# Nine gather slots with four routes in place of ten with three, and adjacency reloads in four parts, in a two-layer graph kernel

## The chip, the cores and the metric

The kernel runs on one core of a Trainium2 chip. The metric is the device time of one execution in microseconds (us).

## The reference

Two layers on N = 4096 nodes with D = 512 features. Cut to what matters:

```python
# layer 0: normalized adjacency, x: (4096, 512), adj: (4096, 4096)
a = adj + eye(N);  d = sum(a, axis=1) ** -0.5
h = relu((d[:, None] * a * d[None, :]) @ x @ W.T + b)
x = layernorm(x + h)
# layer 1: attention of 8 heads, masked by the adjacency
adj = maximum(adj, eye(N))
scores = q @ k.T * kd ** -0.5 + 0.01 * eye(N) - 1e16 * (1 - adj)
x = layernorm(x + sum_over_heads(softmax(scores) @ v @ Wo))
```

The adjacency matrix has a diagonal and some 0.2% of the other entries, all of them below 1. With a mask of 1e16 * (1 - adj), softmax then gives each row its own diagonal, and layer 1 becomes a matrix product with the sum over heads of Wv Wo. Layer 0 needs the few edges of each row only.

## The kernel before

`few_edges_below_one` computes this short form, and at its end a flag `bad` that says whether the inputs allow it (all values below 1, no row segment with too many edges, every edge found a slot). If not, a general kernel runs after it.

The rows are 32 tiles of 128. Five compute engines' queues (PE, DVE, ACT, POOL and SP, which here only issues DMAs) each run in their own order; a tile framework puts in the waits and may move instructions of a queue past each other, except where `keep_in_program_order` is used.

**First stage** (to about 220 us). It loads all adjacency tiles (2 MB each), sums their rows for the degrees, forms y = d * (x W.T) tile by tile and writes y to DRAM. DVE meanwhile begins to extract edges: `extraction` takes for each of eight column segments of a tile the eight largest values (L731) and their places (L732), packs them into keys, sorts out the 24 largest per row, and writes a record `rec` (column, weight, destination row and their remainders in low precision). It handles 7 of a tile's 16 steps per iteration here, and the rest in the second stage. Twelve tiles are extracted early from their first load, five stay resident in SBUF, and the other fifteen (`again`) are loaded a second time in the second stage by `reload` (L535), each into one of the five slots of the pool `big` once an older tile in it is extracted and its negative sum taken (`scan_half`, L687, two halves per tile on ACT).

**Matching.** A row may have more edges than KH = 10 slots. Rows of a tile are ranked by their number of edges (`match_key` L808, `match_across` L815, `match_ranks` L822), and a permutation matrix (`match_perm` L832) with products on PE (`match_move` L840 and L843) brings edges 10 to 23 of the fullest rows into free slots of emptier rows. The constant `sources` says which rank sends to which row; each of the three ROUTES moves a range of slots of the rows from one rank on. `match_end` (L851 to L858) writes the result to `wr_all` (column, weight, row distance, negated weight) and `cols_all`. The stages of this pipeline are issued at fixed steps k of an iteration.

**Second stage** (from about 220 us). Iteration i has KH steps k. In each, PE multiplies the gathered rows g of one slot by a 128x128 matrix s_t (L1265), POOL issues the indirect gather of a slot AHEAD = 18 slots later (L1057), and ACT builds one matrix of a later tile (`spread`, L955 to L968): for the first SAME = 5 slots a scaled identity, for the others a square and a relu that put each weight in its destination row. Around it stand, at steps given by `at`: `load_own` (L1067 and L540: own rows of y and x, two iterations ahead, three buffers), `own_part` (L1115, ACT), `own_bias` (L1119, DVE), `scaled` (L1126) and `residual` (L1137) on DVE at step 1 of the next iteration, four transposes and their copy hT (L663, L668) at step 0 two iterations behind, the product with wvo (`times`, L675) at step 6, the sum of squares (L1145), `variance` (L1156), `power` on POOL for two tiles at once (L1164), and `finish` (L1170 and L1171) for two tiles at once. The last two tiles (SUMMED) add up their first SAME slots on DVE and ACT before one product. The remaining extraction is shared out over 28 iterations (SPREAD). PSUM has eight banks: two for transposes, one (`bank`) for both `match_across` and `match_move`, five for products.

Of the kernel before, what the change touches and what calls it, by code (L numbers as in the profile page):

```python
# [9 lines left out]
FP = mybir.dt.float32  # L10
# [4 lines left out]
P = 128  # L15
# [404 lines left out]
def few_edges_below_one(  # L420
# [32 lines left out]
    KH = 10  # L453

    ROUTES = ((112, 10, 14), (120, 14, 19), (76, 19, 24))
    SAME = KH - max(hi - lo for _, lo, hi in ROUTES)

# [9 lines left out]
    ps_a = ctx.enter_context(tc.tile_pool(name="ps_a", bufs=5, space=bass.MemoryType.PSUM))  # L467
# [34 lines left out]
    for n, (c, _, _) in enumerate(ROUTES):  # L502
        ranks(sources[:, n + 1, : c + 1], -2, 2 * c + 1 - P)
        ranks(sources[:, n + 1, c + 1 :], -2, P - 1)
# [205 lines left out]
    def extraction(t, a_t, rec):  # L710
# [35 lines left out]
        def drop(f, r):  # L746
# [19 lines left out]
                lambda: nc.scalar.activation(  # L766
                    mask, keyf[:, 0], AF.Sign, accum_out=n_all[:, t : t + 1]
                ) if second else nc.vector.tensor_scalar(
                    mask, keyf[:, 0], 0.0, 0.0, op0=ALU.is_gt, op1=ALU.add,
                    accum_out=n_all[:, t : t + 1],  # L770
                ),
# [28 lines left out]
    bank = ps_t.tile([P, 512], FP, name="bank", bufs=1)  # L800
# [12 lines left out]
    def match_across(key):  # L813
        pk = bank[:, :P]
        tc.keep_in_program_order(nc.tensor.transpose(pk, key.to_broadcast([P, P]), ident))  # L815
        return pk
# [18 lines left out]
    def match_move(rec, perm):  # L835

        r = upper(rec)
        merged = bank[:, P : P + 7 * KH].rearrange("p (f k) -> p f k", f=7)
# [3 lines left out]
        for n, (_, lo, hi) in enumerate(ROUTES):  # L842
# [6 lines left out]
    def match_end(t, merged):  # L849
# [5 lines left out]
        if second:  # L855
            nc.scalar.activation(wr[:, 3], wr[:, 1], AF.Copy, scale=-1.0)
        else:
            nc.vector.tensor_scalar(wr[:, 3], wr[:, 1], -1.0, None, op0=ALU.mult)  # L858
# [42 lines left out]
    def steps():  # L901

        after = [[] for _ in range(STEPS)]
        for n, t in enumerate(order):
            if t not in a_tiles:
                reload()
            edges[t] = dict(rec=recs.tile([P, 7, K], FP, name="rec"))
# [32 lines left out]
    reloaded, scanned = [], []  # L940

    def reload():

        t = queue.pop(0)
        reloaded.append(t)
        a_tiles[t] = load_a(t)
# [100 lines left out]
    AHEAD = 18  # L1047
# [14 lines left out]
    def load_own(i):  # L1062
# [3 lines left out]
        yo[i] = p2.tile([P, D], FP, name="yo", bufs=3)  # L1066
        nc.sync.dma_start(yo[i], y[ts(t, P), :])  # L1067
        xs[i] = load_x(t, nc.sync, p2, 3)
# [42 lines left out]
    def own_part(i):  # L1111
        t = order[i]
        own = own_all[:, t : t + 1]
        d = d_all[:, t : t + 1]
        nc.scalar.activation(own, own, AF.Identity, scale=d, bias=d)  # L1115
# [15 lines left out]
    def residual(i, c=slice(0, D), part=0):  # L1131
        if i % 2 == 0 and i not in sts:
            sts[i] = small.tile([P, 2, 5], FP, name="sums")
            sts[i + 1] = sts[i][:, 1]
            pairs[i] = sts[i]
            sts[i] = sts[i][:, 0]
# [23 lines left out]
    def power(i, n):  # L1160

        j = i % 2
        st = pairs[i - j][:, j : j + n]
        nc.gpsimd.tensor_tensor(  # L1164
            st[:, :, 4], st[:, :, 3], mhalf.to_broadcast([P, n]) if n > 1 else mhalf, ALU.pow
        )
# [39 lines left out]
    yo, zs, hs, pts, hTs, ws, sts, pairs, mats, halves = ({} for _ in range(10))  # L1206
# [4 lines left out]
    load_own(1)  # L1211
    own_part(0)
# [8 lines left out]
    def at(step, i, k):  # L1221

        near = {"T": (1, 5), "M": (1, 8), "Q": (2, 2), "V": (2, 3), "F": (2, 7)}
        far = {"T": (2, 0), "M": (2, 6), "Q": (3, 1), "V": (3, 4), "F": (3, 8)}
        for table, tiles in ((near, range(NT - 2, NT)), (far, range(NT - 2))):
            behind, place = table[step]
            if k == place and i - behind in tiles:
                return i - behind
        return None

    for i in range(NT + 2):
# [5 lines left out]
        for k in range(KH):  # L1237
            ends = p == NT - 1
            t = at("T", i, k)
            if t not in (None, NT - 1):  # L1240
                hTs[t] = evacuate(p2, "hT", transpose_rows(hs[t]))
            t = at("M", i, k)
            if t not in (None, NT - 1):
                ws[t] = times(hTs.pop(t), wvo)
            if i == NT - 1:
# [3 lines left out]
                if k == 7:  # L1249
# [105 lines left out]
```

## Time and profile before

| | us |
|---|---|
| median of 3 runs | 749.92 |
| lowest, highest | 746.94, 760.13 |
| the profiled execution | 746.64 |
| its span, first to last instruction | 744.8 |

| engine | busy us | share of the span |
|---|---|---|
| PE | 591.2 | 79% |
| DVE | 545.4 | 73% |
| ACT | 525.2 | 71% |
| POOL | 393.2 | 53% |

The page has busy rows, the span in 40 slices (18.6 us each; a digit is the busy share in tenths), queues, and groups of instructions with their mean duration and what ended the idle time before them. PE is TensorE's matmul row and PEld its weight loads. An fp32 product of 128x512 has two records of each. In lists of waits, "A <- B: total, times, longest" says that the engine of A stood idle before A until B was done; "issue" and "remote" are idle times for which the profile shows no releaser. Shares are means over stages: the first stage and the second have different limits.

### The profile page before, as it was taken

To read this page: it belongs to the slowest core of one execution; us is meant where nothing else is said; L and a number is where in the kernel's file an instruction comes from. 1 tells how busy PE (TensorE), PEld (TensorE's weight loads), DVE (VectorE), ACT (ScalarE), POOL (GpSimd) and SP (SyncE) were. 2 spreads that over 40 slices of the span, in tenths; PEclk is the share of its full clock that TensorE was granted. 3 is DMA by queue.
4 is the path that set the end of the run, shared out by engine and by line. 5 is a ranking of instruction groups with operands and counts; after the bars stand their busy time and mean duration, and the time that the engine had idled before them with its cause. 6 is when DMAs were issued, how large, how long until landed. Compare 5 with 4: busy or idle time off the path is not lost. (4 is left out here: it accounts for less than half of the span.)

```text
span 744.8 us, 8023 instructions
## 1 busy us (share of the span) xinstructions
PE 591.2 (79%) x1638; PEld 273.9 (37%) x1638; DVE 545.4 (73%) x2109; ACT 525.2 (71%) x1152; POOL 393.2 (53%) x494
## 2 busy tenths in 40 slices
PE   1799959867815687989979699979996789898692
PEld 0444424433302233434434344434442334343350
DVE  6779899999997289889978799959994443322410
ACT  1787798958975287688958597867884887773432
POOL 3224233322337656766666666666665566667500
PEclk9999999999967778999999899999998899999896
DMA  8999999999947689999999988989996577777601
GB/s 341 403 422 426 425 423 406 421 430 413 423 187 262 198 294 366 343 371 373 380 305 343 325 300 313 337 297 333 351 333 209 171 221 239 224 240 248 199 24 62
DMA packets 54411, 230.54 MB, mean 310 GB/s; under 512 B 8592, under 2 KB 9616, under 8 KB 48080
## 3 DMA queue, kind: packets, MB, share of 16 engines
q0 software_dynamic: 30800, 100.95, 40.6%
q1 hardware_dynamic: 18416, 119.55, 40.5%
q10 hardware_dynamic: 5136, 9.44, 3.4%
q14 instruction: 44, 0.36, 0.1%
q8 instruction: 15, 0.25, 0.1%
HBM read 213.12 MB, written 16.78 MB: 309 GB/s over the span
## 5 line engine op out<-in xcount | busy, mean ns | idle before, releaser
L1057 POOL DMA_INDIRECT g<-y,cols_all x320 | 312.9, 978 | 151.0 <-issue 82.6
L1265 PE MATMUL acc<-g,s_t 128*128 128x512 f32 x600 | 283.6, 619 | 20.0 <-ACT s_t L959 20.0
L731 DVE MAX8 v_all<-a_t 128x8 f32<-128x512 f32 x256 | 168.8, 679 | 18.1 <-DMA a_t<-in_adj_dram 18.1
L732 DVE FIND_INDEX8 idx<-v_all,a_t 128x8 uint32<-128x512 f32 x256 | 174.0, 683 | 0.0
L1265 PEld LDWEIGHTS acc<-g,s_t 128*128 128x128 f32 x600 | 116.2, 200 | 151.9 <-issue 124.4
L675 PE MATMUL acc<-wvo,hT 128*128 128x512 f32 x256 | 125.4, 630 | 25.4 <-issue 14.8
L675 PE MATMUL acc<-wT,xT 128*128 128x512 f32 x256 | 121.7, 621 | 16.4 <-ACT xT L668 12.2
L687 ACT ACTIVATE dump<-a_t 128x2048 uint8<-128x2048 f32 (+1 forms) x52 | 119.5, 2297 | 0.0
L675 PEld LDWEIGHTS acc<-wvo,hT 128*128 128x128 f32 x256 | 49.1, 200 | 87.6 <-issue 71.9
L675 PEld LDWEIGHTS acc<-wT,xT 128*128 128x128 f32 x256 | 48.3, 198 | 72.3 <-issue 50.2
L955 ACT ACTIVATE sq<-cols,wr_all 128x128 f32<-128x128 f32 x192 | 66.9, 391 | 9.9 <-issue 7.3
L959 ACT ACTIVATE s_t<-sq,wr_all 128x128 f32<-128x128 f32 x160 | 72.0, 483 | 1.6 <-ACT sq L955 1.2
L968 ACT ACTIVATE s_t<-s_t,wr_all 128x128 f32<-128x128 f32 x150 | 52.4, 391 | 4.6 <-issue 3.8
L682 ACT ACTIVATE dump<-a_n 128x4096 uint8<-128x4096 f32 x15 | 54.5, 3632 | 0.3 <-DMA a_n<-in_adj_dram 0.3
L744 DVE MAX8 top<-key 128x8 f32<-128x64 f32 x192 | 39.0, 214 | 12.1 <-issue 7.3
L1119 DVE SCALAR_TENSOR_TENSOR yo<-yo,own_all,b_bc 128x512 f32<-128x512 f32 x32 | 23.8, 744 | 24.1 <-DMA yo<-y 10.4
L1126 DVE SCALAR_TENSOR_TENSOR h<-acc,d_all,yo 128x512 f32<-128x512 f32 (+1 forms) x33 | 23.9, 724 | 23.5 <-PE acc L1265 11.3
L540 POOL DMA_DIRECT2D x_t<-in_x_dram x32 | 17.9, 564 | 41.2 <-PE pt L663 41.0
L694 POOL TENSOR_SCALAR deg<-deg_all 128x1 f32<-128x1 f32 x32 | 6.7, 220 | 62.4 <-ACT dump L682 62.3
L704 POOL DMA_DIRECT2D y<-y_t x32 | 19.0, 593 | 38.6 <-ACT y_t L702 38.1
L702 ACT ACTIVATE y_t<-acc,d_all 128x512 f32<-128x512 f32 x32 | 21.6, 686 | 22.6 <-POOL d_all L697 16.7
L815 PE MATMUL bank<-ident,rank_key 128*128 128x128 f32 x32 | 10.2, 320 | 33.4 <-issue 11.5
(123 smaller groups left out, 651.5 us busy)
## 6 DMA issues: line engine op xcount, KB each, us to landing
a_t<-in_adj_dram SPq DMA_DIRECT2D x30, 2048.0 KB
a_n<-in_adj_dram SPq DMA_DIRECT2D x15, 2048.0 KB
x_t<-in_x_dram POOLq DMA_DIRECT2D x32, 256.0 KB
y<-y_t POOLq DMA_DIRECT2D x32, 256.0 KB
yo<-y SPq DMA_DIRECT2D x32, 256.0 KB
x_t<-in_x_dram SPq DMA_DIRECT2D x32, 256.0 KB
out_dram<-r_t ACTq DMA_DIRECT2D x32, 256.0 KB
g<-y,cols_all POOLq DMA_INDIRECT x320
```

Of the source, the lines that this page charges most:

```text
L675: nc.tensor.matmul(u, srcT[:, dc, :], w[:, dc, :], start=(dc == 0), stop=(dc == ND - 1))
L682: nc.scalar.activation(dump[:, : part.shape[1]], part, AF.Copy, accum_out=dst)
L687: nc.scalar.activation(dump[:, o], a_t[:, o], AF.Relu, scale=-1.0, accum_out=neg_all[:, t, halves[0] : halves[0] + 1],)
L731: long.append(lambda o=o, seg=seg: nc.vector.max(v[:, o], seg))
L732: long.append(lambda o=o, seg=seg: nc.vector.max_index(idx[:, o], v[:, o], seg))
L744: return lambda: nc.vector.max(top[:, f, r * 8 : r * 8 + 8], keyf[:, f])
L955: nc.scalar.activation(sq, cols1, AF.Square, bias=wr[:, 2, k : k + 1])
L959: nc.scalar.activation(s_t[:, k, :], away(), AF.Relu, scale=wr[:, 3, k : k + 1], bias=wr[:, 1, k : k + 1],)
L968: nc.scalar.activation(s_t[:, k, :], s_t[:, KH, :], AF.Copy, scale=wr[:, 1, k : k + 1])
L1057: nc.gpsimd.indirect_dma_start(out=slots[j], out_offset=None, in_=y[:, :], in_offset=bass.IndirectOffsetOnAxis(ap=cols_all[:, t, k : k + 1 ...
L1126: nc.vector.scalar_tensor_tensor(hs[i][:, c], zs[i][:, c], d_all[:, order[i] : order[i] + 1], yo[i][:, c], op0=ALU.mult, op1=ALU.add,)
L1265: nc.tensor.matmul(zs[i], mats[i][:, k, :], slots.pop(i * KH + k), start=(k == 0), stop=(k == KH - 1),)
```

## The change

- KH goes from 10 to 9, so each tile has nine gathers, nine products and nine steps per iteration. Four ROUTES replace three: edges 9 to 12, 13 to 15, 16 to 19 and 20 to 23. `sources` is filled with a value that matches no rank, and 22 runs of destination rows with their first source rank are written into it.
- `match_across` and `match_move` get PSUM tiles of their own, and the products have four banks.
- Some jobs of the second stage go from ACT to DVE: the count of edges (`mask`, L766), the negated weight (L856), and `own_part` (L1115).
- Transposes and their copy are three steps apart, `power` is taken per tile and at step 3, `finish` per tile at step 3 four iterations behind. `load_own` is three iterations ahead with four buffers. AHEAD is 16. The matching stages have other steps.
- A reload is booked at step 8 from iteration 2 on. Its four parts of 512 KB are issued at steps 0, 3, 5 and 7 from the next iteration on, or all at once before the extraction that needs the tile.

```diff
-    KH = 10
-    ROUTES = ((112, 10, 14), (120, 14, 19), (76, 19, 24))
-    SAME = KH - max(hi - lo for _, lo, hi in ROUTES)
+    KH = 9
+    ROUTES = (
+        (9, 13, ((62, 79, 54), (82, 89, 36), (91, 94, 28), (96, 96, 24), (99, 101, 23),
+                 (104, 107, 20), (110, 112, 16), (114, 127, 13))),
+        (13, 16, ((63, 65, 10), (66, 68, 13), (74, 75, 15), (80, 81, 7), (95, 95, 5), (97, 98, 4),
+                  (102, 103, 2), (108, 108, 0))),
+        (16, 20, ((61, 61, 4), (66, 66, 2), (90, 90, 1), (109, 109, 3), (113, 113, 0))),
+        (20, 24, ((109, 109, 0),)),
+    )
+    SAME = KH - max(hi - lo for lo, hi, _ in ROUTES)
...
-    ps_a = ctx.enter_context(tc.tile_pool(name="ps_a", bufs=5, space=bass.MemoryType.PSUM))
+    ps_a = ctx.enter_context(tc.tile_pool(name="ps_a", bufs=4, space=bass.MemoryType.PSUM))
...
-    for n, (c, _, _) in enumerate(ROUTES):
-        ranks(sources[:, n + 1, : c + 1], -2, 2 * c + 1 - P)
-        ranks(sources[:, n + 1, c + 1 :], -2, P - 1)
+    nc.gpsimd.memset(sources[:, 1:], float(P))
+    for n, (_, _, runs) in enumerate(ROUTES):
+        for a, b, r in runs:
+            ranks(sources[:, n + 1, a : b + 1], -2, 2 * r + 1 - P)
...
-                lambda: nc.scalar.activation(
-                    mask, keyf[:, 0], AF.Sign, accum_out=n_all[:, t : t + 1]
-                ) if second else nc.vector.tensor_scalar(
-                    mask, keyf[:, 0], 0.0, 0.0, op0=ALU.is_gt, op1=ALU.add,
-                    accum_out=n_all[:, t : t + 1],
-                ),
+                one(mask, keyf[:, 0], 0.0, 0.0, op0=ALU.is_gt, op1=ALU.add,
+                    accum_out=n_all[:, t : t + 1]),
...
-    bank = ps_t.tile([P, 512], FP, name="bank", bufs=1)
-        pk = bank[:, :P]
+        pk = ps_t.tile([P, 512], FP, name="pk", bufs=1)[:, :P]
-        merged = bank[:, P : P + 7 * KH].rearrange("p (f k) -> p f k", f=7)
+        pm = ps_t.tile([P, 512], FP, name="pm", bufs=1)
+        merged = pm[:, : 7 * KH].rearrange("p (f k) -> p f k", f=7)
...
-        if second:
-            nc.scalar.activation(wr[:, 3], wr[:, 1], AF.Copy, scale=-1.0)
-        else:
-            nc.vector.tensor_scalar(wr[:, 3], wr[:, 1], -1.0, None, op0=ALU.mult)
+        nc.vector.tensor_scalar(wr[:, 3], wr[:, 1], -1.0, None, op0=ALU.mult)
...
             if t not in a_tiles:
                 reload()
+            while t in [u for u, _ in coming]:
+                reload_part()
...
-    reloaded, scanned = [], []
+    reloaded, scanned, coming = [], [], []
+    PARTS = 4
     def reload():
         t = queue.pop(0)
         reloaded.append(t)
-        a_tiles[t] = load_a(t)
+        a_tiles[t] = big.tile([P, N], FP, name="a_t")
+        coming.extend((t, c) for c in range(PARTS))
+    def reload_part():
+        if coming:
+            t, c = coming.pop(0)
+            o = ts(c, N // PARTS)
+            nc.sync.dma_start(a_tiles[t][:, o], adj[ts(t, P), o])
...
-    AHEAD = 18
+    AHEAD = 16
...
-        yo[i] = p2.tile([P, D], FP, name="yo", bufs=3)
+        yo[i] = p2.tile([P, D], FP, name="yo", bufs=4)
-        xs[i] = load_x(t, nc.sync, p2, 3)
+        xs[i] = load_x(t, nc.sync, p2, 4)
...
-        nc.scalar.activation(own, own, AF.Identity, scale=d, bias=d)
+        nc.vector.tensor_scalar(own, own, 1.0, d_all[:, t : t + 1], op0=ALU.add, op1=ALU.mult)
...
-    def power(i, n):
-        j = i % 2
-        st = pairs[i - j][:, j : j + n]
-        nc.gpsimd.tensor_tensor(
-            st[:, :, 4], st[:, :, 3], mhalf.to_broadcast([P, n]) if n > 1 else mhalf, ALU.pow
-        )
+    def power(i):
+        st = sts[i]
+        nc.gpsimd.tensor_tensor(st[:, 4:5], st[:, 3:4], mhalf, ALU.pow)
...
-        near = {"T": (1, 5), "M": (1, 8), "Q": (2, 2), "V": (2, 3), "F": (2, 7)}
-        far = {"T": (2, 0), "M": (2, 6), "Q": (3, 1), "V": (3, 4), "F": (3, 8)}
+        near = {"T": (1, 5), "E": (1, 5), "M": (1, 8), "S": (1, 6), "Q": (2, 2), "V": (2, 3), "F": (2, 7)}
+        far = {"T": (2, 0), "E": (2, 3), "M": (2, 7), "S": (2, 1), "Q": (3, 0), "V": (3, 3), "F": (4, 3)}
...
             if k == 2:
-                load_own(i + 2)
+                load_own(i + 3)
-            if k == 6 and i < NT:
+            if k == 4 and i < NT:
                 own_bias(i)
-            if k == 6 and has_p:
-                eps_var(p)
+            for t in at("S", i, k):
+                eps_var(t)
...
-                match(*{1: (RANKS,), 3: (MOVE, PERM), 6: (END,), 7: (KEY,), 9: (ACROSS,)}.get(k, ()))
+                match(*{2: (RANKS,), 4: (MOVE,), 5: (PERM, KEY), 8: (ACROSS, END)}.get(k, ()))
...
-            if k == 9 and queue and len(reloaded) < free:
+            if k == KH - 1 and i >= 2 and queue and len(reloaded) < free:
                 reload()
+            if k in (0, 3, 5, 7):
+                reload_part()
```

## The prediction

> **What bounds the kernel now.** I read the page first (busy rows and slices), then busy time in one window per iteration of the second stage, then the waits, then the timelines of the engines around its longest iterations.
>
> The page gives no single full engine:
>
> ```profile
> PE 591.2 (79%) x1638; PEld 273.9 (37%) x1638; DVE 545.4 (73%) x2109; ACT 525.2 (71%) x1152; POOL 393.2 (53%) x494
> DMA  8999999999947689999999988989996577777601
> ```
>
> Slices 1 to 11 (to 205 us) are the first stage, under DMA at 9 tenths and more. Only constants change there, so it stays. The second stage runs from the first gather (221.8) to the last product (about 730). I cut it at each start of L1126, which ends an iteration; the columns are PE, PEld, DVE, ACT, POOL, clock, DMA share, GB/s:
>
> ```profile
> 334.10:347.60 13.50, 13.46 (x40) 6.05 (x39) 13.50 (x54) 11.13 (x32) 9.22 (x11) 1.00 0.99 365
> 409.10:427.70 18.60, 12.38 (x36) 6.08 (x36) 14.41 (x49) 10.90 (x35) 12.82 (x13) 0.87 0.93 331
> 440.90:454.20 13.30, 13.30 (x42) 6.29 (x40) 13.28 (x52) 12.05 (x33) 7.90 (x8) 1.00 0.92 334
> 482.80:503.70 20.90, 16.24 (x42) 7.31 (x41) 13.27 (x57) 12.51 (x32) 14.29 (x15) 0.92 0.87 297
> 628.30:644.30 16.00, 14.21 (x37) 6.04 (x35) 5.58 (x28) 14.05 (x41) 11.66 (x13) 1.00 0.73 226
> ```
>
> A good iteration takes 13.3 to 13.5 us, and PE and DVE are then both full. But the mean is 15.6 (19 iterations from 271.9 to 568.6, while DVE still extracts), and 15.1 in the nine after, to 704.4, where DVE is below half. Four of the 19 take 18.6 to 20.9 us, one of the nine 23.7. DVE does about 13.6 us in each of the 19 (257.8 us summed over the windows), long or short: the long ones hold no more work, they hold waits. The waits show which:
>
> ```profile
> POOL sums L1164 <- DVE sums L1156: 36.7, 5, 15.9
> POOL g L1057 <- PE acc L1265: 34.4, 40, 3.0
> ACT wr_all L856 <- DVE wr_all L853: 17.2, 4, 7.0
> ACT r_t L1170 <- POOL sums L1164: 12.0, 4, 6.3
> DVE yo L1119 <- ACT own_all L1115: 8.8, 4, 3.4
> DVE key L747 <- ACT mask L766: 8.5, 3, 6.0
> PE bank L815 <- DVE wr_all L853: 7.2, 3, 4.5
> ```
>
> Each is a tiny instruction on another engine that everything queued behind it must wait for. Two places, from the engines' timelines (start, length, and in brackets the idle time before and its releaser):
>
> ```profile
> 424.31 0.21 ACT L856 ACTIVATE wr_all<-wr_all 128x10 f32<-128x10 f32 x1 [7.03 <-DVE wr_all L853]
> 426.34 0.48 PE L815 MATMUL bank<-ident,rank_key 128*128 128x128 f32 x1 [6.22 <-ACT dump L1145]
> 380.69 1.26 ACT L1170 ACTIVATE r_t<-acc,sums 128x512 f32<-128x512 f32 x2 [6.29 <-POOL sums L1164]
> 385.19 3.67 PE L675 MATMUL acc<-wvo,hT 128*128 128x512 f32 x4 [4.17 <-ACT hT L668]
> ```
>
> At 424 ACT stands 7 us for a sign change of ten numbers, and the rank key that PE wants is behind it. At 380 ACT stands for POOL's power, which is behind a gather that waits for a slot of PE; the copy of hT is behind ACT's output, and PE waits for it: a circle through four queues.
>
> **What the Trainium skill says.** (1) "TensorE: Matmul & The Clock Gate", the section on the array's architecture, says that ACT and DVE queues are strict FIFO; the 7.03 above agrees. (2) "PSUM — Partial Sum Buffer", section on bank collisions, has PSUM guarded by bank rather than by address; the 7.2 us of L815 waiting for L853, two uses of different columns of one bank, agree. (3) "Perfetto Trace Analysis", § Optimizing Scalar/DVE Operations, advises moving work to Scalar where DVE is saturated; this change does the reverse, with DVE at 13.6 of 15.6. (4) The same page, § DMA Optimizations, says that splitting a DMA may let parts start sooner. No part-wise reload exists in this trace.
>
> **The change part by part.** Durations are from the group rows.
>
> *One slot less per tile.* 32 slots go in all.
> - PE: eight L1265 records fill 3.43 us until the next group, 0.43 each, two to a slot, so 0.86 per slot. Per iteration 28 records (20 for slots, 8 for wvo), 12.0, and 1.1 for transposes, key and routes: 13.1 before, 12.3 after. The fourth route adds one small matmul (three take 0.24).
> - POOL: a gather costs 0.95 and 0.30 before the next, 1.25. Ten and half a paired power (0.72) make 13.0. Nine and one power per tile (0.55 plus a gap of 0.3) make 12.1.
> - DMA: q0 moves 100.95 MB in 40.6% of the span, 3.0 us per MB; q1 119.55 MB in 40.5%, 2.5. An iteration with a reload moves 2.62 MB of gathers (7.9), 2.62 of reload, yo and x (6.6) and 0.26 of output (0.7): 15.2 before, 14.4 after.
> - ACT: SAME stays 5, so a square and a relu go per tile: 0.39 + 0.48 = 0.87.
>
> *Four small jobs.* mask to DVE (0.28 by L768 and its read, 18 tiles: 5.0), the negation (0.19, 24 tiles: 4.6), own_part (0.2, 32: 6.6), perm a quarter wider (at most 0.09, 32: 2.9): DVE gains 19 us, about 0.7 per iteration, and ACT loses 7.8 + 4.9 + 12.1 = 25 us. If DVE packs the same extraction into each iteration, its floor becomes 14.3. That is the cost of the waits removed.
>
> *Stages.* PSUM tiles pk and pm replace bank; ps_a goes from 5 to 4. Products live from step 7, two iterations behind, to step 3, four behind, with zs beside them: four at most. The slot that M takes was freed four steps earlier, so I cost it at 0; without that cover PE would wait the rest of a step, 1.4 us. Evacuation stands three steps after the transposes, power a whole iteration before finish: the circle at 380 opens. yo and x come an iteration earlier, which covers the 10.4 us of L1119 waiting for yo. POOL carries 16 more iotas (7 took 1.10, so 2.5 us) and a memset before its x_t loads at 3.4 us; their first reader on PE starts at 25.4, so 0; uncovered, 3.
>
> *Reloads.* The first goes from iteration 1 (issued at 264.6) to iteration 3. SP works in order, and its only brakes are the waits of load_own for the scaled rows, and freed slots. So I expect parts not really spread: three or four in a bunch after each load_own. DVE read the first reloaded tile at about 290 (137 of the 256 MAX8 are done then); its parts would now be issued at 272 to 287. AHEAD falls from 18 to 16: 16 slots at 13.5/9 us are still 24 us of lead. Bounds: a gain of 5 (less burst before the gathers) to a loss of 10; I take a loss of 4 while the lead builds up.
>
> *Sum.* The 19 iterations: four long ones lose about 4.5 each, 18; the other 15, mean 14.5, are held by DVE's floor of 13.6 to 14.3 and come to about 13.9: 9. The nine late ones go from 15.1 to 13.6, PE's 12.3 with a smaller remainder of waits: 13.5. The first two (228 to 272), where ACT stood 9.2 us before L856: 4. The end, two summed tiles with one product less each: 2. Less 4 for reloads: 42.5. The profiled execution took 746.6 us (span 744.8), 3.3 below the median of the three runs, 749.9; so 704 against it, and 708 on the scale of the median.
>
> **The rivals.**
> - *Only the load shrinks.* The waits move but stay as long in total: 30 iterations times about 0.87 of PE and POOL is 26, plus 2 at the end, 721. For it: the late iterations have waits while DVE is idle. Against: the waits above have named causes that go.
> - *DVE takes over.* Extraction keeps its share of every iteration, so 19 iterations have a floor of 13.6 + 0.7 and keep the present unfilled 2.0 us: 16.3, 13 us more; late ones save 9 × 0.87 = 8, start, end and reloads 2. So about 753 on the scale of the median at the worst, 744 if half the unfilled time goes. For it: DVE is full in short iterations. Against: a mean of 2 us idle with its cause on ACT.
> - *Reloads starve DVE* (the slower side). A part is issued after load_own, and one tile per iteration is the most; if DVE reaches a segment before it lands, it stops and its scaled and residual stand behind it, hence PE. Price: the longest present wait of L731 for a tile is 5.7 us; at that for the 15 reloads 86, less 42 of gain and 25 that hides in other waits, 19 lost: 769. It decides once the lead falls below a landing (2.1 MB at 360 GB/s, 6 us). Against: at 13.6 us an iteration DVE reads 0.87 tile and loads bring one, so the lead grows.
> - *The change doesn't do what it says.* If the routes didn't hold every edge, the flag would start the general path: its aggregation alone is 1024 slots of 0.86, 880 us, so over 1,600.
>
> **How the numbers follow.** Forecast 0.61, load only 0.15, DVE 0.13, starvation 0.09, general path 0.02. The likeliest case's own range is 690 to 728. The range 688 to 744 takes in load only and the half-filled DVE case. Two per cent of 749.9 is 15 us, about what this kernel's measurement can tell from no change: faster than 735 has 0.76, within 735 to 765 0.13, slower 0.11.
>
> **What would show it.** 288 gathers; PE's good iterations at 12.3 to 12.6 late, 13.5 to 14 while DVE extracts; ACT's waits for L853 and POOL's power gone from the top; L815's bank wait gone; DVE busy about 19 us more. Wrong, if L731 waits for reloads by over 10 us, if iterations during extraction stay at 15.5 with DVE above 14.3, or if the late nine stay near 15.

## The result, and the profile after

| | before | after |
|---|---|---|
| median us | 753.67 (4 runs, 746.94 to 760.13) | 716.72 (4 runs, 715.35 to 725.36) |
| ratio to before, 95% interval | 1 | 0.9562 (0.9436 to 0.9689) |
| the profiled execution, us | 746.64 | 716.18 |
| its span | 744.8 | 714.4 |

The change makes the kernel 4.4% faster. Of the 42.5 us of the prediction's sum, 30.4 came between the spans of the two profiled executions. (Ratios here and below take only the runs within 1.5% of the fastest of their kernel, so that a ratio can differ from the quotient of the medians.)

The page of the kernel after, its busy row and the DMA row of its slices:

```profile
PE 571.2 (80%) x1604; PEld 263.4 (37%) x1604; DVE 550.9 (77%) x2201; ACT 492.0 (69%) x996; POOL 372.4 (52%) x494
DMA  8999999999963969999999978969889775877611
```

No engine's share has moved by more than four points. The first eleven slices of DMA are as full as they were: the first stage is the same. (Line numbers shift: the products are L1271 now, the gathers L1069, `scaled` L1137, `variance` L1164, `power` L1170, the loads of reload parts L958.)

Cut at each start of `scaled` as before, three windows of the kernel after (PE, PEld, DVE, ACT, POOL, clock, DMA share, GB/s):

```profile
375.40:388.00 12.60, 11.47 (x35) 5.49 (x36) 12.60 (x54) 12.57 (x33) 8.99 (x10) 1.00 0.88 289
437.10:449.80 12.70, 12.70 (x35) 5.95 (x34) 12.70 (x53) 9.73 (x27) 9.40 (x10) 1.00 0.79 268
449.80:468.60 18.80, 14.05 (x41) 5.89 (x39) 12.90 (x46) 9.96 (x27) 9.78 (x11) 1.00 0.71 262
```

A good iteration now takes 12.6 us, where it took 13.4; a long one still takes up to 18.8. Where the 30 us came from, by the marks of both traces:

| stretch | before | after | gain | forecast |
|---|---|---|---|---|
| start to the first mark | 262.2 | 263.0 | -0.8 | 4, with the next iteration |
| first to second mark | 9.7 | 8.2 | 1.5 | |
| the next 19 iterations | 296.7 | 282.1 | 14.6 | 27, less 4 for reloads |
| the nine after these | 135.8 | 127.6 | 8.2 | 13.5 |
| last mark to the end of the span | 40.4 | 33.5 | 6.9 | 2 |

Waits of the kernel after, over the whole run (total, times, longest):

```profile
POOL sums L1170 <- DVE sums L1164: 44.5, 13, 6.3
POOL g L1069 <- PE acc L1271: 16.1, 24, 2.1
...
ACT above L826 <- remote: 19.3, 1, 19.3
DVE v_all L740 <- DMA a_t<-in_adj_dram: 16.4, 5, 5.7
DVE h L1137 <- remote: 15.6, 1, 15.6
```

ACT's waits for DVE's wr_all, for POOL's sums and the waits for mask and own_all, which the prediction was built on, have left the list. In their place POOL stands before `power` for DVE's `variance`: 13 times, where it was five. Between the first and the last mark, power's group row (busy, mean ns, then idle just before it) shows this wait alone:

```profile
L1170 POOL TENSOR_TENSOR sums<-sums,mhalf 128x1 f32<-128x1 f32 x28 | 18.2, 650 | 38.1 <-DVE sums L1164 29.1 <-DVE rec L792 3.5 <-DVE rec L750 1.9
```

The same row of before has 12.0 us of idle for 13 paired powers. One such place is inside the 18.8 us iteration above. POOL's timeline of the kernel after (start, length, and in brackets the idle time before and its releaser):

```profile
460.68 0.95 POOL L1069 DMA_INDIRECT g<-y,cols_all  x1 [0.30 <-issue]
467.93 0.56 POOL L1170 TENSOR_TENSOR sums<-sums,mhalf 128x1 f32<-128x1 f32 x1 [6.30 <-DVE sums L1164]
468.67 0.99 POOL L1069 DMA_INDIRECT g<-y,cols_all  x1 [0.18 <-issue]
```

and DVE's, in the same 6 us:

```profile
463.10 0.69 DVE L741 FIND_INDEX8 idx<-v_all,a_t 128x8 uint32<-128x512 f32 x1
...
467.05 0.68 DVE L740 MAX8 v_all<-a_t 128x8 f32<-128x512 f32 x1
467.65 0.19 DVE L1164 TENSOR_SCALAR sums<-sums 128x1 f32<-128x1 f32 x1
```

For 7 us, from 461.6 to 468.7, POOL issues no gather, because the next thing in its queue is one power of 0.56 us, and the 0.19 us of variance that feeds it stands behind a row of extraction operations in DVE's queue.

But POOL's pause is not what makes this iteration long. ACT and PE stand at the same time, and for something else (ACT's line first, then three of PE):

```profile
470.68 0.20 ACT L1159 ACTIVATE sums<-sums 128x1 f32<-128x1 f32 x1 [9.08 <-DVE h L1145]
...
452.03 4.46 PE L1271 MATMUL acc<-g,s_t 128*128 128x512 f32 x10
...
470.80 1.09 PE L672 MATMUL pt<-ident,h 128*128 128x128 f32 x4 [6.15 <-DVE top L753]
471.68 7.00 PE L1271 MATMUL acc<-g,s_t 128*128 128x512 f32 x10
```

PE's transposes and ACT's sum need the h of a tile. By the order of the program, the products of this tile were done before PE's transposes at 451.57; DVE starts its `scaled` only at 468.64, and the h is complete at 470.65. Until then DVE works at extraction, with pauses of its own: it is busy for 12.9 of the iteration's 18.8 us. When PE goes on, ten product records run in one row, so the gathered rows were there. POOL's pause and PE's end alike with DVE's queue, in which `variance` (467.65) and `scaled` stand one behind the other. And PE's pause costs more than its length. The granted clock is 1.00 from 452.0 to 456.4, where ten such records take 4.46 us, and 0.51 from 469.9 to 476.8, as the pause ends, and ten of them take 7.00.

### The profile page after: what moved, and what is told of

Read it like the earlier page. It is cut to its first block, busy times and chain, and to the rows that moved or that the text cites. A ratio compares the mean times of both kernels' runs of the same rounds, so it can differ in the third digit from the quotient of the medians.

```text
span 714.4 us, 7907 instructions
## 1 busy us (share of the span) xinstructions
PE 571.2 (80%) x1604; PEld 263.4 (37%) x1604; DVE 550.9 (77%) x2201; ACT 492.0 (69%) x996; POOL 372.4 (52%) x494
## 5 line engine op out<-in xcount | busy, mean ns | idle before, releaser
L1069 POOL DMA_INDIRECT g<-y,cols_all x288 | 282.0, 979 | 114.1 <-issue 69.5
L1271 PE MATMUL acc<-g,s_t 128*128 128x512 f32 x540 | 254.5, 609 | 20.0 <-DMA x_t<-in_x_dram 16.0
L740 DVE MAX8 v_all<-a_t 128x8 f32<-128x512 f32 x256 | 172.0, 680 | 17.0 <-DMA a_t<-in_adj_dram 16.4
L684 PE MATMUL acc<-wvo,hT 128*128 128x512 f32 x256 | 135.0, 676 | 43.7 <-ACT hT L677 17.1
L1271 PEld LDWEIGHTS acc<-g,s_t 128*128 128x128 f32 x540 | 100.0, 195 | 131.3 <-issue 112.9
L684 PE MATMUL acc<-wT,xT 128*128 128x512 f32 x256 | 126.6, 644 | 26.8 <-ACT xT L677 16.7
L967 ACT ACTIVATE sq<-cols,wr_all 128x128 f32<-128x128 f32 x160 | 58.4, 391 | 14.4 <-issue 9.9
L971 ACT ACTIVATE s_t<-sq,wr_all 128x128 f32<-128x128 f32 x128 | 58.9, 483 | 1.0 <-ACT sq L967 0.4
L1170 POOL TENSOR_TENSOR sums<-sums,mhalf 128x1 f32<-128x1 f32 x32 | 20.4, 637 | 62.2 <-DVE sums L1164 44.5
L1153 ACT ACTIVATE dump<-acc 128x512 f32<-128x512 f32 x32 | 18.8, 589 | 48.9 <-PE acc L1271 23.7
L980 ACT ACTIVATE s_t<-s_t,wr_all 128x128 f32<-128x128 f32 x150 | 46.9, 390 | 0.0
L1137 DVE SCALAR_TENSOR_TENSOR h<-acc,d_all,yo 128x512 f32<-128x512 f32 (+1 forms) x33 | 23.7, 719 | 21.1 <-remote 15.6
```

The costliest lines, as they stand in the source:

```text
L684: nc.tensor.matmul(u, srcT[:, dc, :], w[:, dc, :], start=(dc == 0), stop=(dc == ND - 1))
L740: long.append(lambda o=o, seg=seg: nc.vector.max(v[:, o], seg))
L967: nc.scalar.activation(sq, cols1, AF.Square, bias=wr[:, 2, k : k + 1])
L971: nc.scalar.activation(s_t[:, k, :], away(), AF.Relu, scale=wr[:, 3, k : k + 1], bias=wr[:, 1, k : k + 1],)
L980: nc.scalar.activation(s_t[:, k, :], s_t[:, KH, :], AF.Copy, scale=wr[:, 1, k : k + 1])
L1069: nc.gpsimd.indirect_dma_start(out=slots[j], out_offset=None, in_=y[:, :], in_offset=bass.IndirectOffsetOnAxis(ap=cols_all[:, t, k : k + 1 ...
```

## The experiments

Each kernel is compared with the kernel before in the same series; ratios have 95% intervals. Each series ran on a chip of its own; on that of the third, before took 710.66 us, against 748.94 and 747.33 in the first two. So ratios are compared across series, and times only within one. That a ratio carries over from chip to chip is an assumption: b_slots, with which most of the second and third series is compared, ran in the first alone.

### First series: one part undone, or one part alone

**u_slots**: the kernel after with ten slots and the old three routes.

```diff
-    KH = 9
-    ROUTES = ((9, 13, ...), (13, 16, ...), (16, 20, ...), (20, 24, ((109, 109, 0),)))
+    KH = 10
+    ROUTES = ((10, 14, ((0, 112, 112), (113, 127, 127))), (14, 19, ((0, 120, 120), (121, 127, 127))),
+              (19, 24, ((0, 76, 76), (77, 127, 127))))
```

> The changed kernel with ten slots and the three old routes; all else stays. Theory M (load and waits share the gain: a slot less takes 0.87 us of PE and POOL out of each iteration, the rest comes from the moved jobs and stages): some 24 us back, 738 to 744, near 741. Theory L (only the load counts): all of it back, 750 or more. Theory W (only the waits count, PE and POOL have room): under 728. 320 gathers, short iterations at 13.2 to 13.4 us instead of 12.5.

Measured: 757.20 us, 1.0182 (1.0143 to 1.0221). Without the slot the rest of the change makes the kernel slower, by 14 us (by 8 from median to median). AHEAD stays at 16 here, where before has 18, and no run tests that alone; PE and its weight loads wait 8 us for gathered rows between the marks, 6 in before. The slot brings 1.0182 - 0.9562 = 0.062, 46 us, give or take 10. Theory L, that only the load brings something, stands; the prediction's own (M), in which the removed waits bring their share, falls, and so does W.

**b_slots**: the kernel before with nine slots and four routes, and what the number of steps drags along, nothing else.

```diff
-    KH = 10
-    ROUTES = ((112, 10, 14), (120, 14, 19), (76, 19, 24))
+    KH = 9
+    ROUTES = ((9, 13, ...), (13, 16, ...), (16, 20, ...), (20, 24, ...))
-    AHEAD = 18
+    AHEAD = 16
-                match(*{1: (RANKS,), 3: (MOVE, PERM), 6: (END,), 7: (KEY,), 9: (ACROSS,)}.get(k, ()))
+                match(*{1: (RANKS,), 3: (MOVE, PERM), 6: (END,), 7: (KEY,), 8: (ACROSS,)}.get(k, ()))
...
```

> The kernel before with nine slots and the four routes alone (AHEAD 16 and the last step numbers follow from nine steps; the matching of the last tiles is pulled forward as in the changed kernel). Theory M: 24 us less than before, 726 to 733. Theory L: 717 to 720, the whole gain. Theory W: 742 to 750. The waits of ACT for L853's result and for POOL's power stay in the list under M.

Measured: 699.48 us, 0.9404 (0.9334 to 0.9473), beyond even the 717 to 720 that theory L gave it. The slot alone is worth 45 us here too, and the whole change is 0.016 (12 us, give or take 11) worse than this part of it. What its waits show is as telling as its time:

```profile
POOL g L1066 <- PE acc L1274: 36.3, 36, 4.5
...
ACT wr_all L865 <- DVE wr_all L862: 23.9, 8, 7.6
...
PEld bank L824 <- DVE wr_all L862: 12.8, 5, 4.4
```

ACT's wait for the sign change is longer than before (23.9 against 17.2), the bank wait is there, and the kernel is 6% faster. These waits stood in the profile, and the gain came without their going.

**u_jobs**: the kernel after with mask, negation and own_part back on ACT.

```diff
-                one(mask, keyf[:, 0], 0.0, 0.0, op0=ALU.is_gt, op1=ALU.add, accum_out=n_all[:, t : t + 1]),
+                lambda: nc.scalar.activation(mask, keyf[:, 0], AF.Sign, accum_out=n_all[:, t : t + 1]) if second else ...
-        nc.vector.tensor_scalar(wr[:, 3], wr[:, 1], -1.0, None, op0=ALU.mult)
+        if second:
+            nc.scalar.activation(wr[:, 3], wr[:, 1], AF.Copy, scale=-1.0)
+        else: ...
-        nc.vector.tensor_scalar(own, own, 1.0, d_all[:, t : t + 1], op0=ALU.add, op1=ALU.mult)
+        nc.scalar.activation(own, own, AF.Identity, scale=d, bias=d)
```

> The changed kernel with mask, negated weight and own_part back on ACT in the second stage. Theory M: the waits come back on ACT, some 6 us, 721 to 725. Theory W: 15 us, 730 or more. Theory D (DVE became the bound, so its 16 us of extra work cost something): faster, 703 to 712. Theory L: 715 to 718.

Measured: 703.56 us, 0.9444 (0.9384 to 0.9503). Theory D had 703 to 712. It is 0.012 below the ratio of after, 9 us; the two intervals overlap, so by the times alone this gain is likely and not certain. Its power row, between the marks:

```profile
L1178 POOL TENSOR_TENSOR sums<-sums,mhalf 128x1 f32<-128x1 f32 x27 | 16.2, 599 | 14.4 <-DVE sums L1172 8.5 <-DVE key L744 2.8 <-DVE wr_all L861 1.8
```

The idle time there falls from 38.1 to 14.4 us, and the 29 iterations from 418.0 to 398.1 us.

**u_reload**: the kernel after with whole reloads from the first possible iteration.

```diff
-        a_tiles[t] = big.tile([P, N], FP, name="a_t")
-        coming.extend((t, c) for c in range(PARTS))
+        a_tiles[t] = load_a(t)
-            if k == KH - 1 and i >= 2 and queue and len(reloaded) < free:
+            if k == KH - 1 and queue and len(reloaded) < free:
```

> The changed kernel with whole reloads of 2 MB, booked from the first iteration in which one is possible and issued at step 8. Theory of the prediction (parts go out in bunches behind load_own, and the later start costs about 4): 711 to 717. Rival R (parts shorten the bursts in front of gathers): 722 to 730. L740 waits for reloads stay under 3 us in the second stage in both.

Measured: 710.64 us, 0.9511 (0.9455 to 0.9567), against 0.9562 for after: no difference that these intervals show, and no gain from the parts. SP's timeline of the kernel after says why they change little:

```profile
264.87 1.66 SPq L958 DMA_DIRECT2D a_t<-in_adj_dram  x3
...
273.37 10.93 SPq L958 DMA_DIRECT2D a_t<-in_adj_dram  x5
...
292.49 6.27 SPq L958 DMA_DIRECT2D a_t<-in_adj_dram  x5
...
304.88 5.47 SPq L958 DMA_DIRECT2D a_t<-in_adj_dram  x4
```

Three to five parts go out between two loads of own rows, the first two to four of them within some 2 us, much as predicted, so that they come nearly as a whole tile does.

### Second series: one load added to b_slots

b_slots is the plainest kernel with nine slots. Each of these adds one thing per iteration whose result isn't used.

**x_gather**: one more gather per tile.

```diff
+            if k == 4 and i + 1 < NT:
+                gx = p2.tile([P, D], FP, name="gx", bufs=2)
+                nc.gpsimd.indirect_dma_start(
+                    out=gx, out_offset=None, in_=y[:, :],
+                    in_offset=bass.IndirectOffsetOnAxis(ap=cols_all[:, order[i + 1], 0:1], axis=0),
+                )
```

> Nine slots alone (b_slots) plus one more gather per tile into a buffer that nothing reads: POOL gets its 1.25 us per iteration back and DMA its 256 KB, PE, ACT and DVE nothing. Theory P (POOL or DMA paces the second stage): 31 gathers of 1.25 us, 30 to 39 more than b_slots, 730 to 738. Theory E (PE paces): under 5 more, 698 to 705. Theory C (all queues are coupled and each share costs a part): 8 to 18 more, 707 to 718.

Measured: 739.73 us, 0.9876 (0.9833 to 0.9919): 0.047 above b_slots, 35 us, give or take 6. Thirty-one gathers at 1.25 us are 39, and theory P had 30 to 39. The 1.25 can be read from POOL's timeline of b_slots, where one gather follows another:

```profile
503.54 0.95 POOL L1066 DMA_INDIRECT g<-y,cols_all  x1 [0.30 <-DMA g<-y,cols_all]
504.79 0.95 POOL L1066 DMA_INDIRECT g<-y,cols_all  x1 [0.30 <-issue]
```

The sum fits, but the way to it is not that of P. If POOL were late with its gathers, PE would wait for their rows. The waits for gathered rows between the marks of x_gather are these:

```profile
PEld acc L1274 <- DMA g<-y,cols_all: 2.7, 9, 0.5
```

They are 2.7 us in all, and 4.1 in b_slots. Nor does every iteration grow by 1.25 us. The framework moved the added gathers together: ten of the 31 lie in three iterations (295.8 to 358.4), and these take 62.6 us where the same three of b_slots take 43.1, nearly half of the 42 us by which the two profiles differ between the marks. Of these 42, 13 are PE's: it is busy for 367.3 us against 354.4 with the same products, at a mean granted clock of 0.91 against 0.96. So a gather more is dear, and how its cost reaches the end stays open.

**x_prod**: one more product per tile, with a matrix of zeros.

```diff
+    zero = const.tile([P, P], FP, name="zero")
+    nc.gpsimd.memset(zero, 0.0)
...
+                if k == 4:
+                    nc.tensor.matmul(zs[i], zero, slots[i * KH + k], start=False, stop=False)
```

> Nine slots alone (b_slots) plus one more product per tile (a zero matrix with a gathered slot, two records of 0.43 us) for the 30 tiles that are not summed: PE alone gets the tenth slot's time. Theory E (PE paces): 0.86 times 30, 24 to 28 more than b_slots, 723 to 728. Theory P: under 5 more. Theory V (DVE paces while it extracts, in 23 of the iterations): 3 to 8 more. Theory C: 8 to 15 more.

Measured: 715.89 us, 0.9557 (0.9505 to 0.961): 0.015 above b_slots, 11 us of the 26 that the products last. It isn't a clean price of a product either: in its profile POOL stands 33.6 us before power between the marks, against 8.3 in b_slots.

```profile
L1175 POOL TENSOR_TENSOR sums<-sums,mhalf 128x2 f32<-128x2 f32 x13 | 9.4, 720 | 33.6 <-DVE sums L1167 8.7 <-DVE top L755 8.6 <-DVE rec L804 8.3
```

So a part of the 11 us, possibly all, is that wait, and the product's own share stays open.

**x_dve**: one more operation of about 0.7 us on DVE per iteration.

```diff
+            if k == 3 and has_p and not ends:
+                dx = p2.tile([P, D], FP, name="dx", bufs=1)
+                nc.vector.scalar_tensor_tensor(dx, hs[p], 0.0, xs[p], op0=ALU.max, op1=ALU.add)
```

> Nine slots alone (b_slots) plus one DVE operation of 128x512 per iteration (0.7 us, its result unused), behind the residual of the tile before. Theory V (the order of the queues fills DVE, so what is added to DVE lengthens the stage): 15 to 22 more than b_slots, 714 to 722. Theory E and P: under 5 more, since DVE has a quarter of the stage free. Theory C: 6 to 13 more.

Measured: 700.38 us, 0.9357 (0.9307 to 0.9408). No cost is seen in the whole time, though DVE is full in the short iterations: theory V with its 15 to 22 us falls. In the profile the 29 iterations do take 407.2 us against 397.8 of b_slots, which an earlier first mark (254.4 against 260.0) and a shorter end hide, so a cost below V's isn't excluded.

**x_act**: one more square and relu on ACT per tile.

```diff
+            if k == 3 and i + 1 < NT:
+                wx = wr_all[:, order[i + 1]]
+                sx = mat.tile([P, P], FP, name="sx", bufs=2)
+                nc.scalar.activation(sx, cols1, AF.Square, bias=wx[:, 2, KH - 1 : KH])
+                sy = mat.tile([P, P], FP, name="sy", bufs=1)
+                nc.scalar.activation(sy, sx, AF.Relu, scale=wx[:, 3, KH - 1 : KH], bias=wx[:, 1, KH - 1 : KH])
```

> Nine slots alone (b_slots) plus the square and the relu of one more slot per tile on ACT (0.87 us per iteration), its result unused. Theory C: 5 to 12 more than b_slots. Theories E, P and V: under 4 more, 697 to 704.

Measured: 687.05 us, 0.9184 (0.9136 to 0.9232). More work and 2.2% less time than b_slots. No theory had that. It is the measure of caution for all the rest: an added operation also changes where the queues' orders meet, and that alone was worth some 16 us here. The differences for the gather (35 us) and for the slot (45 and 46 us, in two bases) are well above it; the 9 to 14 us of the jobs, the powers and the parts aren't.

### Third series: bytes or instructions, and the jobs alone

**x_small**: the added gather fetches 32 numbers per row instead of 512, 16 KB instead of 256.

```diff
-                gx = p2.tile([P, D], FP, name="gx", bufs=2)
-                    out=gx, out_offset=None, in_=y[:, :],
+                gx = p2.tile([P, 32], FP, name="gx", bufs=2)
+                    out=gx, out_offset=None, in_=y.rearrange("n (a b) -> (n a) b", b=32),
```

> Nine slots alone (b_slots) plus one more gather per tile as in x_gather, but of 32 numbers per row instead of 512: POOL issues 31 gathers more, DMA moves 16 KB each instead of 256 KB. Theory P1 (POOL's issue of gathers paces): as x_gather, some 35 to 40 more than b_slots, 735 to 740. Theory P2 (DMA's bytes pace): under 12 more, which is what a change of the order alone has given, 695 to 711.

Measured: 704.11 us, 0.9904 (0.9874 to 0.9935), no cheaper than x_gather's 0.9876. The group rows of the added gathers, x_gather's first (count, busy us, mean ns):

```profile
L1282 POOL DMA_INDIRECT gx<-y,cols_all x31 | 30.5, 983 | 22.3 <-issue 8.5 <-DVE cols_all L863 3.7 <-DVE idx L741 2.9
```

and x_small's:

```profile
L1282 POOL DMA_INDIRECT gx<-y,cols_all x31 | 31.1, 1004 | 12.0 <-issue 5.2 <-DMA gx<-y,cols_all 3.8 <-DMA g<-y,cols_all 1.2
```

A sixteenth of the bytes, and the same 1.0 us of POOL each. The bytes are not what is paid for. But here too the cost comes in few places: the fifth iteration takes 33.6 us, and most of the others in which DVE extracts take 12.1 to 13.5. Six of the added gathers fall into that one iteration. Power stands behind five of them in POOL's queue, and ACT stands before its output until power is done. That wait is ACT's longest between the marks:

```profile
ACT r_t L1179 <- POOL sums L1173: 70.9, 11, 23.6
```

For the last 17 of these 23.6 us POOL issues gathers one after the other. In x_dma, next, the same wait comes to 29.6 us in 7 times. In b_slots (6.0) and x_gather (4.0), on other chips, it is short, so the cost need not go the same way there.

**x_dma**: 256 KB more per iteration by the program, loaded by SP in one plain DMA instead of a gather.

```diff
+            if k == 4 and has_p and not ends:
+                gx = p2.tile([P, D], FP, name="gx", bufs=2)
+                nc.sync.dma_start(gx, y[ts(order[p], P), :])
```

> Nine slots alone (b_slots) plus one plain load of 256 KB of y per iteration on SP's queue, which nothing reads: DMA gets the bytes of the tenth gather back, POOL nothing. Theory P2 (DMA's bytes pace): 20 to 35 more than b_slots, 720 to 735. Theory P1 (POOL's issue paces): under 12 more, 695 to 711.

Measured: 670.82 us, 0.944 (0.9411 to 0.9468), beside b_slots' 0.9404: no cost that the intervals show. The DMA issues of x_dma list the added loads (count, size, us from issue to landing), and the view of their line has the first and last start (after the least, median and longest issue in ns):

```profile
gx<-y SPq DMA_DIRECT2D x31, 256.0 KB, 7.4
...
L1302 SPq DMA_DIRECT2D gx<-y x31: 319/320/572, 224.8 to 349.4; - x31
```

The loads were not spread as meant: SP ran ahead, and all of them are issued by 349.4, in the first eight iterations after the first mark or before it. Those eight take 122.2 us, against 110.7 in b_slots (on another chip) and 110.3 in b_jobs below; the other 21 take 267.6, against 287.1 and 264.7. So a cost of some 12 us where the loads run isn't excluded. P2's 20 to 35 us do not come. Within this series, on one chip, 31 gathers of 16 KB (x_small) cost 33 us more than 31 plain loads of 256 KB. As far as these two runs go, what is paid for in a gather is above all its instruction in POOL's queue, not its bytes.

**b_jobs**: b_slots with the three jobs on DVE, powers still in pairs and all other steps as before.

```diff
+                one(mask, keyf[:, 0], 0.0, 0.0, op0=ALU.is_gt, op1=ALU.add, accum_out=n_all[:, t : t + 1]),
...
+        nc.vector.tensor_scalar(wr[:, 3], wr[:, 1], -1.0, None, op0=ALU.mult)
...
+        nc.vector.tensor_scalar(own, own, 1.0, d_all[:, t : t + 1], op0=ALU.add, op1=ALU.mult)
```

> Nine slots alone (b_slots) with mask, negated weight and own_part moved to DVE as in the change, and nothing else. Theory J (the jobs on DVE cost time by their place, whatever surrounds them): 9 to 17 more than b_slots, 708 to 717. Theory O (the 13 us between the changed kernel and u_jobs came from the order of the queues): within 6 of b_slots, or faster. My prediction's own reason (the moved jobs end waits on ACT): 5 to 20 faster.

Measured: 659.56 us, 0.9296 (0.9263 to 0.9329), better than before, and by ratio than after and b_slots, which didn't run on this chip. The jobs on DVE don't cost as such (theory J falls); here they go with a gain of 0.011, which is no larger than what x_act showed an order of queues to be worth. The page of b_jobs:

```profile
PE 549.2 (84%) x1604; PEld 258.1 (39%) x1604; DVE 545.0 (83%) x2201; ACT 487.9 (74%) x996; POOL 362.9 (55%) x479
```

**u_jobs_reload**: the kernel after with both the jobs and the reloads undone (the two diffs above).

> The changed kernel with the three jobs back on ACT and with whole reloads from the first possible iteration. If both costs are real and add: 13 and 6 less than the changed kernel, 694 to 701, level with b_slots. If the reload's 6 came from the order of the queues: 701 to 708, as u_jobs.

Measured: 665.18 us, 0.9366 (0.9334 to 0.9397). Adding up the two single steps gives 0.9562 - 0.0118 - 0.0051 = 0.9393; within its interval the two steps add up.

### The wait before power, over all kernels

Between the first and the last mark (29 iterations), from the windows and the waits of each trace. "POOL taken" is POOL's busy time and the gaps of "issue" before its instructions, as a share.

| kernel | us | PE busy | DVE busy | POOL taken | idle before power, us |
|---|---|---|---|---|---|
| before | 442.2 | 86% | 72% | 83% | 12.0 |
| u_slots | 442.0 | 87% | 73% | 86% | 37.1 |
| after | 418.0 | 87% | 77% | 81% | 38.1 |
| u_reload | 421.3 | 88% | 77% | 81% | 40.1 |
| x_prod | 418.1 | 90% | 74% | 80% | 33.6 |
| u_jobs | 398.1 | 88% | 79% | 85% | 14.4 |
| b_slots | 397.8 | 89% | 79% | 85% | 8.3 |
| x_dve | 407.2 | 88% | 81% | 83% | 14.2 |
| x_act | 386.9 | 91% | 80% | 84% | 4.6 |
| x_gather | 439.5 | 84% | 72% | 84% | 8.0 |
| third series: x_small | 417.5 | 88% | 75% | 85% | 0.3 |
| x_dma | 389.8 | 93% | 80% | 82% | 1.3 |
| b_jobs | 374.9 | 94% | 84% | 86% | 5.5 |
| u_jobs_reload | 386.3 | 92% | 81% | 83% | 0.6 |

Of the kernels with nine gathers above the third series, those with 34 to 40 us of this wait take 418 to 421 us, those with 5 to 14 take 387 to 407. The wait and the lost time go together. That the wait is the cause isn't shown: between the marks of after, PE and its weight loads wait 1.5 us in all for gathered rows, and neither ACT nor DVE waits for power at all. In the long iteration above the wait was a sign of DVE's lateness, like PE's pause. What brings the wait about is less clear still. In the kernel after, power stands in the same step as variance and directly behind it, once per tile, and the jobs on DVE make its queue longer; with the jobs gone (u_jobs), or with paired powers (b_jobs, on the other chip), the wait is short. But x_prod has it with paired powers and the jobs on ACT. The powers alone were not changed in any run, so this part is argued from the profiles and not shown. The table has one profiled execution per kernel; that of u_reload is 7 us above its median, that of u_slots 6 below.

## Why the prediction was right, and which of its terms were wrong

Faster came, and 716.7 lies in the range, 9 us above the centre. That it is so close is luck, for two terms were wrong in opposite directions: the slot brought 17 us more than its 28, and the rest lost 12 us where it was to gain 14.5.

**What a slot is worth: too small by some 17 us.** The rival of the load alone put 26 us on the slot in 30 iterations and 2 at the end, 0.87 us each, which is the slot's time on PE at full clock; the sum uses the same prices, and what is left of its 42.5 is the 14.5. Measured: 46 us (u_slots) and 45 us (b_slots), 1.5 us per iteration. The failing step is the choice of the engine to price it by. POOL's 1.25 us per gather was worked out in the prediction and then used only as a load of 13.0 to 12.1 per iteration, below the iterations' length. In the runs an added gather costs 35 us, an added product 11 with another wait in it. The page misled here: it has POOL at 53%, the lowest of the four compute engines, while between the marks of before POOL is taken 83% of the time, if the 0.30 us before each gather is counted with it. That POOL's full queue sets the pace isn't shown, though: PE doesn't wait for its rows. The price per product also left out the clock. Two of the long iterations in the prediction's own windows have 0.87 and 0.92 there, and a pause that goes may take slow products behind it along; how much of the 45 us that is, no run shows. "DMA: Bandwidth & Descriptors" in the Trainium skill, § SWDGE vs HWDGE vs iDMA, says that for a DMA issued from GpSimd a core computes the descriptors in software; that the same 128 rows cost POOL 0.98 us with 256 KB and 1.00 with 16 KB agrees.

**What the removed waits are worth: not 18 us.** The four long iterations of before were said to be long by ACT's waits (at 424 and 380), the mask, own_part and the bank, and to lose 4.5 us each. The waits did leave the list, and the long iterations stayed: six of the 19 still last 17 us or more. b_slots keeps those very waits, more of the first than before had, and is faster than after. The failing step is from "ACT stood 7 us here" to "the iteration is 4.5 us longer for it". Why these pauses of ACT cost so little is open; no run isolates it.

**The single power: priced by its own time only.** It was costed at 0.55 plus 0.3 per tile, and the circle at 380 was to open. For ACT it did: its wait for POOL's sums is gone. But the prediction did not ask what power itself waits for, though the first row of its list of waits was exactly that, POOL for DVE's variance (most of it at the end of the kernel). That wait between the marks went from 12.0 to 38.1 us. Whether it cost anything itself is open (PE's rows were there). The rest of the change, which the sum had at 14.5 us of gain (42.5 less 28), costs 14 us at ten slots (u_slots) and 12, with its wide interval, at nine.

**Iterations, one by one.** Good ones were to take 12.3 to 12.6 late and 13.5 to 14 while DVE extracts; the good ones take 12.3 to 12.9 while DVE extracts, and the three shortest late ones 10.1 to 12.7. The floor of 14.3 on DVE was wrong: DVE holds 12.7 us per iteration while it extracts, where it held 13.6, since the same extraction spreads to iteration 24 instead of 20. x_dve's added 0.7 us are not seen in the whole time. The extraction's mean went from 15.6 to 14.8 only, and so came near to the mark of 15.5 that was to count as a refutation. The nine late ones went from 15.1 to 14.2, where 13.6 was forecast.

**Small terms.** DVE was to gain 19 us and gained 5.5 on the page: the negation has a median of 0.16 us and own_part of 0.20 there, and consecutive small operations overlap in the records, so that busy time grows less than their sum (all of DVE's durations together grow by 13.4 us). ACT fell by 33 us. The first two iterations were to gain 4 and gained 0.6: DVE and ACT stand idle before the first mark, of which below. The end gave 6.9 where 2 was forecast, and no run took it apart. The reloads' loss of 4 is neither shown nor excluded (u_reload's 0.0051, inside the intervals); the bunches behind each load of own rows came as described. Of the stated signs, the 288 gathers are there:

```profile
L1069 POOL DMA_INDIRECT g<-y,cols_all x288 | 282.0, 979 | 114.1 <-issue 69.5
```

**The rivals.** "Only the load shrinks" (721) ends nearest to the measured 716.7, but not for its reason: the load alone is worth 45 us, and the waits did not just stay, a new one came. "DVE takes over" falls in its size, with x_dve and b_jobs: moving work from ACT to a busier DVE cost nothing that shows where the powers stayed paired. But DVE can hold the others up: in the long iteration shown above PE and ACT wait for it, though it is busy for 12.9 of the 18.8 us. "Reloads starve DVE" did not happen: between the marks the list of waits has none of DVE for a tile of the matrix, and over the whole run there are 16.4 us where before had 18.1. The general path did not start: the gathers are 288 and the span is what it is.

## What to carry to other kernels

Price a removed step on every queue that serves it, with the gaps between its instructions counted, and test the prices by adding one such step: here the dearest was the gather, on the queue with the lowest busy share. Then look where the added instructions really ran, for a framework or a queue that runs ahead can bunch them. A long wait in the profile is worth only what a kernel without it gains, and the cheapest test is a kernel that keeps the wait and changes the load. Before a wait is called the cause, ask who waited for the engine that stood. When a tiny instruction is moved, look up first what it waits for, and where its producer stands in its own queue.

## What the runs showed of the hardware, not expected

- An indirect gather of 128 rows takes POOL about 1.0 us and 0.30 before the next, whether it fetches 2 KB or 128 bytes per row (x_gather 983 ns, x_small 1004 ns).
- Thirty-one plain loads of the same 256 KB from SP add nothing that can be seen to the whole time (x_dma 0.944, b_slots 0.9404), though b_slots' DMA share between the marks is already 0.87; in the eight iterations where they run, a cost of some 12 us isn't excluded.
- After PE stood for 6.2 us in the kernel after, its granted clock was 0.51 for the next stretch (469.9 to 476.8), and ten product records took 7.00 us in place of 4.46.
- The kernel before takes 747 to 749 us in the first two series and 711 in the third. The ratios of like experiments agree between them (x_gather 0.9876, x_small 0.9904), the times don't. A part of the difference lies in the first stage: the first mark is at 254 to 266 us in the traces of the first two series and at 240 to 249 in those of the third.
- At the start of the second stage DVE and ACT stand, in both kernels (ACT's `above` waits 12.4 us in before). The first `scaled` of after waits 15.6 us (and `above` on ACT 19.3, in the waits above), with no releaser in the trace:

```profile
262.99 0.75 DVE L1137 SCALAR_TENSOR_TENSOR h<-acc,d_all,yo 128x512 f32<-128x512 f32 x1 [15.61 <-remote]
```

Its cause stays open. The first mark came no earlier than in before, and with it the gain of the first iterations was missed.
